# Selective scan of a 2D state-space layer: tiles of four states by 32 channels in place of two by 64, on one core

## The chip, the cores and the metric

The kernel runs on one core of a Trainium2 chip. The metric is the device time of one execution in microseconds. Five engines work side by side and meet only through semaphores: PE (TensorE, matrix products into PSUM), DVE (VectorE), ACT (ScalarE), POOL (GpSimd) and SP (SyncE, which here only issues DMAs, in the order of the program).

## The reference, cut to what matters

Two layers work on 8 images of 64 x 64 tokens with 192 channels. Layer 0 is not touched. Layer 1 projects to 384 channels, convolves, and runs a selective scan in four directions over the 4096 tokens. For each direction `k`, channel `d` and state `n` of 16:

```
x_dbl = x_proj_weight[k] @ xs[k]            # 12 rows for delta, 16 for B, 16 for C
delta = softplus(dt_projs_weight[k] @ x_dbl[:12] + dt_projs_bias[k])
A     = -exp(A_logs)
# per token l, sequential:
h[d, n] = exp(delta[d, l] * A[d, n]) * h[d, n] + (delta[d, l] * u[d, l]) * B[n, l]
y[d, l] = sum over n of h[d, n] * C[n, l]
ys      = y + u * Ds
```

The four directions (rows, columns, and both backwards) are summed, normalized over channels, gated and projected back. All arithmetic is in float32.

## The kernel before, in words

`layer1` handles one image after another. `front` (projection, convolution, stores of the result by channels and by tokens to DRAM, `xo`) and `finish` of the image before are interleaved by a planner; then `main` runs the scan of the image, which is the part that the change rewrites. Its order is written out by hand.

A **step** is one direction and one stretch of 512 tokens: 4 x 8 = 32 steps an image, 256 in all. A step has 24 **units**. A unit is two tiles `f` of 128 partitions by 512 tokens. Before the change a unit is `(p, d)`: `p` is a pair of the 16 states, `d` one of three groups of 128 channels, and each of the unit's two tiles holds 2 states x 64 channels. `ORDER` interleaves the eight `p`.

For each unit these are issued, unit `u` being the loop's index:

- `run(u)`: two scans on DVE (`tensor_tensor_scan`, line 1662) over decay `ea` and supply `g`, then on POOL a copy of the last column as the carry (`cy`, 1674) and the product of the states with C (`hs`, 1676; C is spread over partitions by DMA in the tile `cb`).
- `decay(u + 2)`: on ACT, two exponentials (1620) of `dr` (delta repeated over partitions by DMA) into `ea`, of which there are three buffers.
- `weigh`: on ACT (1605), delta times u, turned so that tokens lie on partitions (`duT`), is scaled with one state's B into `pw`; some are issued ahead for the next `p`.
- `supply(u + 1)`: on PE, `pw` is transposed into the PSUM tile `g` in blocks of 128 tokens (1646). For the first block of the four later `p`, `on_diagonal` holds: there, B has been laid on the diagonal of a 128 x 128 matrix `dg`, and a product of `duT` with it (1634) takes the place of `weigh` and transpose. `g` has four buffers.
- `collect(u - 2)`: on PE (1691), `sel` sums the product over the states of a tile into the PSUM tile `y`, 64 output channels at a time. In direction 0 the term `u * Ds` is added there too (`dskip`).
- `add(u - 3)`: on DVE (1700, 1702), after the last `p`, `y` goes into the image's sum.

Beside that, the pieces of `prepare(s + 1)` are issued at fixed units `q` of step `s`. At q = 0 `load` issues the DMAs of the next step's input, `xc` (1469) by channels and `ut` by tokens. At q = 2, 3, 4 `project` (1488) multiplies `xc` on PE, at q = 5 `keep` copies the result and stores C to DRAM (`cd`, 1497), and `spread` writes B to the diagonal of a DRAM matrix `dz` (1502) and reads it back as `dg` (1503). At q = 7 to 17 come delta (softplus on ACT), its transposes and `keep_du` (delta times u). `repeat_delta` (1587) spreads delta over the partitions of `dr`, at q = 11, 20 and 21, with four DMAs each. `load_c` (1593) is called at the first unit of each `p`, for the next `p`, with two DMAs into `cb`, of which there are three buffers.

All DMAs of the scan are issued by SP, in the order of the program. A DMA whose target buffer is still in use holds SP, and every DMA behind it, until it is free.

Of the kernel before, what the change touches and what calls it, by code (L numbers as in the profile page):

```python
# [29 lines left out]
NP1 = N // 2  # L30
ND = 8
ORDER = [0, 4, 1, 5, 2, 6, 3, 7]
# [1001 lines left out]
def layer1(tc, consts, x1s, mv1, out, w_in, w_x, w_dt, w_out):  # L1034
# [7 lines left out]
    with ExitStack() as ctx:  # L1042
# [17 lines left out]
        an = wp.tile([128, K, NP1, 2 * DT], F32, name="an")  # L1060
# [6 lines left out]
        sel = wp.tile([128, 64], F32, name="sel")  # L1067
        for i in range(2):
            nc.vector.tensor_copy(sel[i * 64 : i * 64 + 64], ident[i * 64 : i * 64 + 64, i * 64 : i * 64 + 64])
# [24 lines left out]
        zero = yacc[:, 0, : ND * 128].rearrange("p (n b) -> p n b", b=128)  # L1094
        nc.gpsimd.memset(zero, 0.0)
        dzs = [dgp.tile([ND, 128 * 128], F32, name=f"dz{i}") for i in range(2)]
        for t in dzs:
            nc.sync.dma_start(out=t.rearrange("n (a b) -> a n b", b=128), in_=zero)
# [343 lines left out]
        def scan(xo):  # L1442
# [11 lines left out]
            units = [(s, p, d) for s in range(len(steps)) for p in ORDER for d in range(DT)]  # L1454
# [6 lines left out]
            def prepare(s, bank=lambda name: mp.tile([128, TT], F32, name=name, tag="mm")):  # L1461
# [5 lines left out]
                def load():  # L1467
                    st["xc"] = pools["pr1"].tile([128, DT, TT], F32, name="xc")
                    o(nc.sync.dma_start(out=st["xc"], in_=xo[k % 2][:, :, c * TT : c * TT + TT]))
                    st["ut"] = pools["pr1"].tile([128, NB1, DIN], F32, name="ut", bufs=1)  # L1470
                    if k % 2 == 0:
                        src = xo[2][c * TT : c * TT + TT].rearrange("(j p) m -> p j m", p=128)
                        o(nc.sync.dma_start(out=st["ut"], in_=src))
                    else:
                        for i in range(2):
                            src = xo[2].rearrange("(h w) m -> w h m", w=WI)[c * RT + i : c * RT + RT : 2]
                            o(nc.sync.dma_start(out=st["ut"][i * 64 : i * 64 + 64], in_=src.rearrange("j h m -> h j m")))
                    if first(s):
                        st["wd"] = pools["pr1"].tile([45, DIN], F32, name="wd", bufs=1)
                        o(nc.sync.dma_start(out=st["wd"][32:45], in_=w_dt[k]))  # L1480
                    else:
                        st["wd"] = state[s - 1]["wd"]
# [16 lines left out]
                def spread():  # L1499
                    dz = dzs[s % 2]  # L1500
                    st["dg"] = dg = pools["dg1"].tile([128, ND, 128], F32, name="dg")
                    o(nc.sync.dma_start(out=dz[:, :: 128 + 1], in_=xds[s % 2][N - ND : N, 0:128]))
                    o(nc.sync.dma_start(out=dg, in_=dz.rearrange("n (a b) -> a n b", b=128)))
# [11 lines left out]
                def keep_b():  # L1515
                    st["bt"] = bt = pools["pr1"].tile([128, NB1, N], F32, name="bt")
                    o(nc.vector.tensor_copy(bt.rearrange("p a b -> p (a b)"), st["p_b"][:, : NB1 * N]))
                    st["duT"] = pools["pr1"].tile([128, NB1, DIN], F32, name="duT")
# [31 lines left out]
                def keep_du(d):  # L1550
                    o(
                        nc.vector.tensor_mul(  # L1552
                            st["duT"][:, :, d * 128 : d * 128 + 128],
                            st["p_du", d].rearrange("p (j t) -> p j t", j=NB1),
                            st["ut"][:, :, d * 128 : d * 128 + 128],
                        )
                    )
# [12 lines left out]
                    11: [(delta, 1), (turn, 0), (repeat_delta, s, 0)],  # L1570
# [5 lines left out]
                    17: [(keep_du, 2)],  # L1576
                    20: [(repeat_delta, s, 1)],
                    21: [(repeat_delta, s, 2)],
                }

            def repeat_delta(s, d):

                state[s]["dr", d] = dr = pools["dr1"].tile([128, 2, TT], F32, name="dr")
                de = state[s]["de", d]
                for f in range(2):
                    for i in range(2):
                        o(nc.sync.dma_start(out=dr[i * 64 : i * 64 + 64, f], in_=de[f * 64 : f * 64 + 64]))

            def load_c(s, p):
                state[s]["cb", p] = cb = pools["bc1"].tile([128, TT], F32, name="cb")  # L1590
                for i in range(2):
                    o(
                        nc.sync.dma_start(
                            out=cb[i * 64 : i * 64 + 64], in_=state[s]["cd"][2 * p + i].partition_broadcast(64)
                        )
                    )

            def weigh(s, p, j, i):

                st = state[s]  # L1600
                if i == 0:
                    st["pw", p, j] = pools["pw1"].tile([128, 2 * DT, 2, 64], F32, name="pw")
                n = 2 * p + i
# [3 lines left out]
                        st["duT"][:, j].rearrange("p (g c) -> p g c", c=64),  # L1607
# [5 lines left out]
            def decay(u):  # L1613
                s, p, d = units[u]
                k, c = steps[s]
                made["e", u] = ea = pools["e1"].tile([128, 2, TT], F32, name="ea")
                for f in range(2):
                    at = 2 * d + f
                    o(
                        nc.scalar.activation(  # L1620
                            ea[:, f], state[s]["dr", d][:, f], AF.Exp, scale=an[:, k, p, at : at + 1]
                        )
                    )

            def supply(u):
                s, p, d = units[u]
                gs = [pools["g1"].tile([128, TT], F32, name="g") for f in range(2)]
                made["g", u, 0], made["g", u, 1] = gs
                for j in range(NB1):
                    if on_diagonal(p, j):  # L1630
                        for f in range(2):
                            for i in range(2):
                                o(
                                    nc.tensor.matmul(  # L1634
                                        gs[f][i * 64 : i * 64 + 64, j * 128 : j * 128 + 128],
                                        state[s]["duT"][:, j, (2 * d + f) * 64 : (2 * d + f) * 64 + 64],
                                        state[s]["dg"][:, 2 * p + i - (N - ND)],
                                        start=True,
                                        stop=True,
                                    )  # L1640
                                )
                for f in range(2):
                    for j in range(NB1):
                        if not on_diagonal(p, j):
# [3 lines left out]
                                    state[s]["pw", p, j][:, 2 * d + f].rearrange("p a b -> p (a b)"),  # L1648
# [4 lines left out]
            def run(u):  # L1653
                s, p, d = units[u]
                k, c = steps[s]
                st = state[s]
                ea, g = made.pop(("e", u)), [made.pop(("g", u, f)) for f in range(2)]
                h = pools["h1"].tile([128, 2, TT], F32, name="hs")
                rev = (lambda ap: ap) if k < 2 else (lambda ap: ap[:, ::-1])
                for f in range(2):  # L1660
# [4 lines left out]
                            rev(g[f]),  # L1665
                            0.0 if first(s) else state[s - 1]["cy"][:, p, d, f : f + 1],
# [4 lines left out]
                if "cy" not in st:  # L1671
                    st["cy"] = pools["pr1"].tile([128, NP1, DT, 2], F32, name="cy")
                last = TT - 1 if k < 2 else 0
                o(nc.gpsimd.tensor_copy(st["cy"][:, p, d], h[:, :, last]))  # L1674
# [3 lines left out]
            def collect(u):  # L1678
                s, p, d = units[u]
                k, c = steps[s]  # L1680
                st = state[s]
                if p == ORDER[0]:
                    st["y", d] = pools["y1"].tile([128, TT], F32, name=f"y{d}")
                y = st["y", d]
                hc = made.pop(("hc", u))
                half = [slice(f * 64, f * 64 + 64) for f in range(2)]
                if p == ORDER[0] and k == 0:
                    for f in range(2):
                        o(nc.tensor.matmul(y[half[f]], dskip[:, d, half[f]], st["xc"][:, d], start=True, stop=False))
                for f in range(2):  # L1690
                    o(nc.tensor.matmul(y[half[f]], sel, hc[:, f], start=p == ORDER[0] and k > 0, stop=p == ORDER[-1]))  # L1691

            def add(u):
                s, p, d = units[u]
                k, c = steps[s]
                if p == ORDER[-1]:
# [7 lines left out]

            def on_diagonal(p, j):
                return j == 0 and 2 * p >= N - ND
# [4 lines left out]
                for p in ORDER  # L1711
                for j in range(NB1)
                for i in range(2)
# [3 lines left out]
            def prologue(f, mq, front_pools):  # L1717
# [3 lines left out]
                for name, n in (("pr1", 2), ("dr1", 4), ("pw1", 8), ("bc1", 3), ("e1", 3)):  # L1721
# [8 lines left out]
                r = yield step("DVE", 0.7, ready["keep"])  # L1730
                f.give("mm", r)
# [6 lines left out]
                load_c(0, ORDER[0])  # L1738
                for d in range(DT):
                    yield "wait", ("du", d)  # L1740
                for t in todo[:10]:
# [4 lines left out]
            def prologue_of(f, d):  # L1746
# [9 lines left out]
                yield step("SP", 0.1, lambda: repeat_delta(0, d), r)  # L1756
# [7 lines left out]
            def main():  # L1764
                for name, n, kw in (("dg1", 2, {}), ("h1", 6, {}), ("y1", 1, dict(space=PSUM)), ("g1", 4, dict(space=PSUM))):
                    spool(name, n, **kw)
                ready["spread"]()
                supply(0)
                rest = iter(todo[10:])
                nu = len(units)  # L1770
                for u, (s, p, d) in enumerate(units):
                    q = u % (NP1 * DT)
                    if q == 0:
                        pieces = prepare(s + 1) if s + 1 < len(steps) else {}
                    s2, p2, _ = units[u + DT - d] if u + DT - d < nu else (len(steps), 0, 0)
                    if s2 < len(steps) and d == 0:
                        load_c(s2, p2)
# [3 lines left out]
                    for _ in range(((2, 2, 2) if on_diagonal(p, 0) else (3, 3, 2))[d]):  # L1781
# [95 lines left out]
def _layout(i):  # L1877
# [15 lines left out]
    al = l1("A_logs").reshape(K, 2 * DT, 64, NP1, 2).transpose(4, 2, 0, 3, 1)  # L1893
# [39 lines left out]
```

## Time and profile before

| | |
|---|---|
| median of 3 runs | 23168.04 us (23161.08 to 23168.58) |
| profiled execution, its own time | 23175.73 us |
| its span | 23174.0 us |
| mean granted TensorE clock | 0.971 |
| instructions | 348545 |
| DMA packets | 1738653, 1998.38 MB |
| layer 0, and start of layer 1 (first scan of line 1662) | up to about 5023 us |
| scan loops of the 8 images | about 2030 us each |

The profile lists busy time for each engine, the span in slices, the DMA queues, the chain of work that ended last, and groups of instructions with their mean time. Matmuls overlap, so their mean time is longer than the distance from one to the next. SP is not counted as busy; what it does is read from the timeline, where its DMA issues stand as SPq.

### The profile page before, as it was taken

Reading aid. Unit: us, or ns where it says so; the run is one execution under the profiler, and the core shown is the slowest. Engines: PE = TensorE matmul, PEld = TensorE weight load, DVE = VectorE, ACT = ScalarE, POOL = GpSimd, SP = SyncE. Lnnn points to the kernel's source line nnn. Section 1 sums busy time; section 2 is a strip of 40 time slices with the busy share of each in tenths; the row PEclk is TensorE's granted clock in tenths of the full one; section 3 lists DMA queues with packets and bytes.
Section 4 is the critical chain, followed back from the end, with each engine's and each line's share of the span. In section 5 each row is a group of like instructions: output and inputs, shape, how many; then the busy total and the mean of one; then the engine's idle time right before and its main releaser. Section 6 shows DMA issues by size and latency. Waiting matters only on the chain.

```text
span 23174.0 us, 348545 instructions
## 1 busy us (share of the span) xinstructions
PE 21762.7 (94%) x118788; PEld 11070.5 (48%) x118788; DVE 21110.3 (91%) x22093; ACT 20048.9 (87%) x35418; POOL 16109.5 (70%) x12872
## 2 busy tenths in 40 slices
PE   8999999979998999899999999999999999999999
PEld 4444444435554555455545544554455445544554
DVE  7888888869998999899989998999899989998998
ACT  5666666759997999799979997999899989988998
POOL 1111111139995999599959995999599869976997
PEclk8999999989999999999999999999999999999999
DMA  1111111133333333333333334333433343333332
GB/s 52 45 44 41 45 45 45 42 96 92 95 93 111 92 92 94 111 94 93 90 114 93 92 87 117 95 92 88 117 92 92 89 117 93 93 91 113 92 94 75
DMA packets 1738653, 1998.38 MB, mean 86 GB/s; under 512 B 537280, under 2 KB 1034848, under 8 KB 1727648
## 3 DMA queue, kind: packets, MB, share of 16 engines
q1 hardware_dynamic: 1736864, 1976.07, 31.9%
q8 instruction: 934, 15.30, 0.3%
q14 instruction: 855, 7.00, 0.1%
HBM read 1360.20 MB, written 212.60 MB: 68 GB/s over the span
## 4 chain that ended last, share of the span: by engine, by line
PE 48%; ACT 22%; DVE 11%; POOL 8%; issue 6%; DMA 3%; SPq 2%; DVEq 0%; POOLq 0%; ACTq 0%
PE g L1646 10%; PE y L1691 10%; ACT ea L1620 10%; ACT pw L1605 9%; POOL hs L1676 7%; DVE hs L1662 3%; PE g L1634 3%; PE p_f L957 3%; DVE xs L1209 3%; PE p_d L1488 2%; PE p_x L450 2%; PE p_f L977 2%; PE p_dt L1523 2%; DMA dr<-de 2%; PE p_o L874 2%
## 5 line engine op out<-in xcount | busy, mean ns | idle before, releaser
L1676 POOL TENSOR_TENSOR hs<-hs,cb 128x1024 f32<-128x1024 f32 x6144 | 14584.3, 2374 | 496.4 <-POOL cy L1674 4.2
L1662 DVE TENSOR_TENSOR_SCAN hs<-ea,cy,g 128x512 f32<-128x512 f32 x10752 | 12894.9, 1258 | 187.2 <-PE g L1646 178.1
L1620 ACT ACTIVATE ea<-dr,an 128x512 f32<-128x512 f32 x12288 | 8139.8, 710 | 528.5 <-DVE hs L1662 507.0
L1605 ACT ACTIVATE pw<-duT,bt 128x384 f32<-128x384 f32 x14336 | 7832.7, 600 | 23.5 <-DVE duT L1552 23.5
L1691 PE MATMUL y<-hs,sel 128*64 128x512 f32 x24576 | 6635.2, 618 | 360.0 <-POOL hs L1676 338.6
L1646 PE MATMUL g<-ident,pw 128*128 128x128 f32 x43008 | 6089.9, 281 | 41.1 <-ACT pw L1605 4.8
L1646 PEld LDWEIGHTS g<-ident,pw 128*128 128x128 f32 x43008 | 4612.5, 141 | 2522.6 <-issue 1254.9
L1674 POOL COPY cy<-hs 128x2 f32<-128x2 f32 x6144 | 1160.7, 189 | 2262.0 <-DVE hs L1662 2228.8
L1634 PEld LDWEIGHTS g<-dg,duT 128*64 128x64 f32 x24576 | 1557.4, 136 | 2053.0 <-issue 1484.6
L1634 PE MATMUL g<-dg,duT 128*64 128x128 f32 x24576 | 2257.9, 282 | 169.4 <-DVE hs L1662 106.1
L1691 PEld LDWEIGHTS y<-hs,sel 128*64 128x64 f32 x24576 | 1234.2, 135 | 1563.0 <-issue 865.6
L1662 DVE TENSOR_TENSOR_SCAN hs<-ea,g 128x512 f32<-128x512 f32 x1536 | 1751.8, 1197 | 129.1 <-PE g L1646 116.8
L367 POOL TENSOR_TENSOR s<-xs 96x512 f32<-96x512 f32 x64 | 121.7, 1902 | 2139.6 <-DVE xs L345 1850.2
L1523 PE MATMUL p_dt<-xdbl,wd 13*128 13x512 f32 x1536 | 857.5, 639 | 96.2 <-DVE duT L1552 71.0
L1209 DVE SCALAR_TENSOR_TENSOR xs<-pad,p,xs 128x4096 f32<-128x4096 f32 x192 | 860.9, 4484 | 50.7 <-ACT xs L1199 43.5
L367 POOL TENSOR_TENSOR s<-sq 96x512 f32<-96x512 f32 x128 | 180.1, 1407 | 942.7 <-ACT sq L380 864.4
L1488 PE MATMUL p_d<-xc,wx 128*44 128x512 f32 x1536 | 788.6, 596 | 19.9 <-DMA xc<-xo 19.9
L957 PE MATMUL p_f<-h,wf 96*128 96x512 f32 x1536 | 762.4, 635 | 44.1 <-ACT zs L552 27.5
L345 DVE SCALAR_TENSOR_TENSOR x<-xx,p,x 96x512 f32<-96x512 f32 x1024 | 784.8, 816 | 15.2 <-ACT x L334 15.0
L345 DVE SCALAR_TENSOR_TENSOR xs<-xin,p,xs 96x512 f32<-96x512 f32 x1024 | 746.1, 768 | 3.6 <-ACT xs L334 3.6
L977 PE MATMUL p_f<-m,wf 128*96 128x512 f32 x1536 | 696.1, 604 | 0.0
L1545 PEld LDWEIGHTS p_du<-ident,de 128*128 128x128 f32 x3072 | 323.9, 141 | 610.1 <-DVE de L1536 406.3
(205 smaller groups left out, 19972.1 us busy)
## 6 DMA issues: line engine op xcount, KB each, us to landing
cb<-cd SPq DMA_DIRECT2D x4096, 128.0 KB
dr<-de SPq DMA_DIRECT2D x3072, 128.0 KB
xc<-xo SPq DMA_DIRECT2D x256, 768.0 KB
dg<-dz SPq DMA_DIRECT2D x256, 512.0 KB
e<-csd SPq DMA_DIRECT2D x256, 384.0 KB
xl<-x SPq DMA_DIRECT2D x256, 384.0 KB
ut<-xo SPq DMA_DIRECT2D x128, 768.0 KB
ut<-xo SPq DMA_DIRECT2D x256, 384.0 KB
```

Of the source, the lines that this page charges most:

```text
L345: nc.vector.scalar_tensor_tensor(im(out[:, ct]), tap(ct, j), w[:, ct, j : j + 1], im(out[:, ct]), ALU.mult, ALU.add)
L957: nc.tensor.matmul(ps, wf1[:, ct, mt * 128 : mt * 128 + 128], h[:, ct], start=ct == 0, stop=ct == 1)
L1209: nc.vector.scalar_tensor_tensor(xs, tap(j), kw[:, d, j : j + 1], xs, ALU.mult, ALU.add)
L1488: nc.tensor.matmul(st["p_d"][:44], wx[:, d, k], st["xc"][:, d], start=d == 0, stop=d == DT - 1)
L1523: nc.tensor.matmul(ps, st["wd"][32:45, d * 128 : d * 128 + 128], xds[s % 2][32:45], start=True, stop=True)
L1605: nc.scalar.activation(st["pw", p, j][:, :, i], st["duT"][:, j].rearrange("p (g c) -> p g c", c=64), AF.Copy, scale=st["bt"][:, j, n : n + 1],
L1620: nc.scalar.activation(ea[:, f], state[s]["dr", d][:, f], AF.Exp, scale=an[:, k, p, at : at + 1])
L1634: nc.tensor.matmul(gs[f][i * 64 : i * 64 + 64, j * 128 : j * 128 + 128], state[s]["duT"][:, j, (2 * d + f) * 64 : (2 * d + f) * 64 + 64], ...
L1646: nc.tensor.transpose(gs[f][:, j * 128 : j * 128 + 128], state[s]["pw", p, j][:, 2 * d + f].rearrange("p a b -> p (a b)"), ident,)
L1662: nc.vector.tensor_tensor_scan(rev(h[:, f]), rev(ea[:, f]), rev(g[f]), 0.0 if first(s) else state[s - 1]["cy"][:, p, d, f : f + 1], ALU.mu ...
L1676: o(nc.gpsimd.tensor_mul(h, h, bc(st["cb", p], 1, [128, 2, TT])))
L1691: o(nc.tensor.matmul(y[half[f]], sel, hc[:, f], start=p == ORDER[0] and k > 0, stop=p == ORDER[-1]))
```

## The change

A tile now holds 4 states x 32 channels. A unit is `(p, g)`: `p` one of four groups of four states (in plain order), `g` one of six groups of 64 channels, so there are still 24 units of two tiles in a step.

- `supply`: the diagonal is used for one of the four token blocks of `p` = 0 and 2 and for two of them for `p` = 1 and 3 (six of the sixteen pairs of `p` and block, before: four of 32). A tile's diagonal block is made of four products of 32 columns, at column positions 0, 32, 64 and 96, in place of two of 64.
- `weigh` writes four states of 32 channels; the number of its calls in a step is 64 less 4 for each block on a diagonal.
- `collect` works on every second unit: four products with a `sel` of 32 columns, side by side, give 128 channels of `y`.
- `repeat_delta` is called for each of six `g`, at q = 17 to 22, with eight DMAs of 32 partitions each; `dr` has six buffers.
- `load_c` is called for each of four `p`, at units 0, 6, 12 and 18 for the `p` after; it issues four DMAs of 32 partitions into `cb` (now two buffers), and one or two DMAs for `dg`, which is no longer read in `spread`.
- `spread` writes 16 rows of the first block's diagonal and twice four of the second's, in three DMAs. `ut` is gone: `load` reads into `duT`, and `keep_du` multiplies in place.

```diff
-            units = [(s, p, d) for s in range(len(steps)) for p in ORDER for d in range(DT)]
+            units = [(s, p, g) for s in range(len(steps)) for p in range(NQ1) for g in range(NG)]
...
-                    st["dg"] = dg = pools["dg1"].tile([128, ND, 128], F32, name="dg")
-                    o(nc.sync.dma_start(out=dz[:, :: 128 + 1], in_=xds[s % 2][N - ND : N, 0:128]))
-                    o(nc.sync.dma_start(out=dg, in_=dz.rearrange("n (a b) -> a n b", b=128)))
+                    for j, dz in enumerate(dzs[s % 2]):
+                        for p in range(j, NQ1, j + 1):
+                            n = slice(0, N) if j == 0 else slice(4 * p, 4 * p + 4)
+                            o(nc.sync.dma_start(out=dz[n, :: 128 + 1], in_=xds[s % 2][n, j * 128 : j * 128 + 128]))
+                            if j == 0:
+                                break
...
-                    11: [(delta, 1), (turn, 0), (repeat_delta, s, 0)],
+                    11: [(delta, 1), (turn, 0)],
...
-                    17: [(keep_du, 2)],
-                    20: [(repeat_delta, s, 1)],
-                    21: [(repeat_delta, s, 2)],
+                    17: [(keep_du, 2), (repeat_delta, s, 0)],
+                    **{17 + g: [(repeat_delta, s, g)] for g in range(1, NG)},
...
-            def repeat_delta(s, d):
+            def repeat_delta(s, g):
...
                 for f in range(2):
-                    for i in range(2):
-                        o(nc.sync.dma_start(out=dr[i * 64 : i * 64 + 64, f], in_=de[f * 64 : f * 64 + 64]))
+                    at = (2 * (g % 2) + f) * 32
+                    for i in range(4):
+                        o(nc.sync.dma_start(out=dr[i * 32 : i * 32 + 32, f], in_=de[at : at + 32]))
...
+                for i in range(4):
+                    o(nc.sync.dma_start(out=cb[i * 32 : i * 32 + 32], in_=st["cd"][4 * p + i].partition_broadcast(32)))
+                st["dg", p] = dg = pools["dg1"].tile([128, 2, 4, 128], F32, name="dg")
+                for j in range(p % 2 + 1):
+                    src = dzs[s % 2][j][4 * p : 4 * p + 4].rearrange("n (a b) -> a n b", b=128)
+                    o(nc.sync.dma_start(out=dg[:, j], in_=src))
...
+                            for i in range(4):
                                 o(
                                     nc.tensor.matmul(
-                                        gs[f][i * 64 : i * 64 + 64, j * 128 : j * 128 + 128],
-                                        state[s]["duT"][:, j, (2 * d + f) * 64 : (2 * d + f) * 64 + 64],
-                                        state[s]["dg"][:, 2 * p + i - (N - ND)],
+                                        gs[f][i * 32 : i * 32 + 32, j * 128 : j * 128 + 128],
+                                        st["duT"][:, j, at : at + 32],
+                                        st["dg", p][:, j, i],
                                         start=True,
                                         stop=True,
+                                        tile_position=(0, i * 32),
                                     )
                                 )
...
+                hc = [made.pop(("hc", u - 1)), made.pop(("hc", u))]
+                for i in range(4):
+                    o(
+                        nc.tensor.matmul(
+                            y[i * 32 : i * 32 + 32],
+                            sel,
+                            hc[i // 2][:, i % 2],
+                            start=p == 0 and k > 0,
+                            stop=p == NQ1 - 1,
+                            tile_position=(0, i * 32),
+                        )
+                    )
...
             def on_diagonal(p, j):
-                return j == 0 and 2 * p >= N - ND
+                return j <= p % 2
...
-                for name, n in (("pr1", 2), ("dr1", 4), ("pw1", 8), ("bc1", 3), ("e1", 3)):
+                for name, n in (("pr1", 2), ("dr1", 6), ("pw0", 3), ("bc1", 2), ("e1", 3), ("dg1", 2)):
...
-                    s2, p2, _ = units[u + DT - d] if u + DT - d < nu else (len(steps), 0, 0)
-                    if s2 < len(steps) and d == 0:
-                        load_c(s2, p2)
+                    if g == 0 and u + NG < nu:
+                        load_c(*units[u + NG][:2])
                     run(u)
                     if u + 2 < nu:
                         decay(u + 2)
-                    for _ in range(((2, 2, 2) if on_diagonal(p, 0) else (3, 3, 2))[d]):
+                    for _ in range(((1, 1, 2, 2, 1, 1), (1, 2, 3, 2, 2, 2))[p % 2][g]):
                         if t := next(rest, None):
                             weigh(*t)
```

## The prediction

> **What bounds the kernel now.** I read first the busy times of the page, then a stretch in the middle of a scan, then the timeline there, and last what SP waits for.
>
> ```profile
> PE 21762.7 (94%) x118788; PEld 11070.5 (48%) x118788; DVE 21110.3 (91%) x22093; ACT 20048.9 (87%) x35418; POOL 16109.5 (70%) x12872
> ```
>
> Over the span PE looks busiest. Inside the scan (windows: for each engine busy us and instructions) it is DVE:
>
> ```profile
> core 0: us, PE busy (x) PEld busy (x) DVE busy (x) ACT busy (x) POOL busy (x), PEclk, DMA share, GB/s
> 8500.00:9000.00 500.00, 482.61 (x3088) 252.16 (x3084) 495.51 (x471) 491.51 (x878) 480.72 (x383) 1.00 0.36 94
> ```
>
> DVE is idle 0.9% of this stretch. From the starts of every 48th scan in the trace, a step lasts 62.9 us in directions 1 to 3 and 65.2 us in direction 0; the idle time before DVE's instructions is 0.34 and 2.34 us of these. So DVE's own work is 62.56 us a step (62.86 in direction 0): a floor, since the change leaves DVE 48 scans and 11 other instructions. POOL's 24 pairs of carry and product, 2.585 us from one to the next, make 62.0. All idle of DVE in the 256 steps is about 349 us, 1.5% of the time: no more can be gained.
>
> Then the timeline, first SP's issues (start, us from the first's start to the last's end, number):
>
> ```profile
> 8517.49 0.59 SPq L1469 DMA_DIRECT2D xc<-xo  x1
> 8536.00 0.33 SPq L1497 DMA_DIRECT2D cd<-xdbl  x1
> 8536.38 0.32 SPq L1502 DMA_DIRECT2D dz<-xdbl  x1
> ```
>
> and, near the end of that step, all engines:
>
> ```profile
> 8568.27 16.50 DVE L1662 TENSOR_TENSOR_SCAN hs<-ea,cy,g 128x512 f32<-128x512 f32 x14
> ...
> 8572.11 2.41 SPq L1587 DMA_DIRECT2D dr<-de  x4
> 8573.48 0.87 PE L1646 MATMUL g<-ident,pw 128*128 128x128 f32 x6
> 8574.28 1.08 PE L1691 MATMUL y<-hs,sel 128*64 128x512 f32 x4
> 8574.61 1.18 SPq L1593 DMA_DIRECT2D cb<-cd  x2
> 8575.19 0.70 PE L1634 MATMUL g<-dg,duT 128*64 128x128 f32 x8
> 8575.90 3.23 SPq L1587 DMA_DIRECT2D dr<-de  x4
> 8579.24 1.19 SPq L1593 DMA_DIRECT2D cb<-cd  x2
> 8580.47 0.60 SPq L1469 DMA_DIRECT2D xc<-xo  x1
> ...
> 8589.49 0.12 PEld L1488 LDWEIGHTS p_d<-xc,wx 128*44 128x44 f32 x1 [0.28 <-issue]
> ```
>
> The two `xc` loads are one step apart (62.98 us). A unit of two scans takes 16.50/7 = 2.36 us. The last `xc` is issued behind eight `dr` and four `cb` DMAs; in nine steps that I followed in the records it landed 5.2 to 6.9 us after its issue began, here 5.2, at 8585.7, and its first product's weights load on PE at 8589.49: 3.8 us to spare. Back to back, DMAs of 64 partitions end 0.64 us apart, whatever they carry (`dr` after `dr`, `cb` after `cb`, `xc` after `cb`, all 0.64 in the issue records). And SP is not free to run ahead:
>
> ```profile
> SPq L1593 <- POOL cy L1674: 4308.7, 1033, 7.6
> ```
>
> (SP's waits: total us, times, longest): `cb` loads wait for POOL to be done with the buffer.
>
> **The change, part by part.**
>
> *ACT.* A step's `weigh` calls fall from 56 to 40. One costs 7832.7 us / 14336 = 0.55: 8.7 us a step less. DVE is the floor, so this is worth only what it saves of DVE's idle. The weights are now finished just before the first `supply` of a `p`: at the end of a step two `weigh` (1.1 us) follow `decay` (1.32) before a transpose (0.17 + 0.3) may run, 2.9 us against a unit of 2.36: up to 0.6 us, four places a step, three of them beside a 0.66 us extra on DVE. I take 0.3 a step, outside the stall below.
>
> *PE.* Pairs of 64 columns run as one: in the records their starts are 7 ns apart, and the next round follows 0.109 us later (128 columns) or 0.43 (512). A tile's diagonal block is two rounds, 0.22, a transpose 0.109. If four groups of 32 run as one, such a block stays at two rounds; 48 more blocks in place of 48 transposes cost 48 x 0.11 = 5.3 us a step, and `collect` falls from 24 to 12 times (0.86 + 0.2 for the switch of shape): -12.7. PE gains 7 us, off the path except in direction 0, where its extra sums cause the 2 us of idle. If four run two at a time the block is 0.44 and `collect` 1.72: see the second rival. The nearest row (pairs do not queue at all) is why I take four at once. The Trainium skill (TensorEngine Tiling (Array Packing), Tiling Modes) also lists four independent tiles of 128 x 32; no run here shows them yet.
>
> *`keep_du`, the carry, the adds, `ut`:* the same instructions with the same shapes; nothing. SP's wait of 3.3 us between `dz` and `dg` goes; SP was idle then.
>
> *SP.* This is the step that decides. DMAs a step: `dr` 12 to 48, `cb` 16 to 16, `dg` 1 to 6, `dz` 1 to 3. Their order around the step's end is now: `dr` of g 0; at unit 18 `load_c` for the next step's `p` 0 (4 `cb`, 1 `dg`); five times eight `dr`; at the next step's unit 0 `load_c` for `p` 1 (4 `cb`, 2 `dg`); only then `xc`. `cb` has two buffers now, so the load at unit 18 waits until POOL has done unit 17, which in the records of before is 2.9 us after that unit's scan ends, i.e. after the start of unit 18. From there 48 DMAs of 32 partitions and three `dg` (0.43 each, 0.386 plus the gap) come ahead of `xc`.
>
> What does one DMA of 32 partitions take on SP? No row shows one. From below: a `dz` behind the 16-partition `cd` ends 0.37 us after it; the shortest single issue of all, 0.305, with its gap 0.35. From above: 0.64, the same DMAs of 64 partitions. By partitions the form lies between, so I take the middle, 0.50. (The data bound each lower: 2 KB packets from SBUF to SBUF take 166 ns on each of 16 engines, two each, 0.33 us.) The Trainium skill (DMA: Bandwidth & Descriptors, Issuing engines are not separate DMA queues) holds the time to initiate a DMA to be usually small beside the DMA itself; by that rule the 0.33 of data would bind and the stall below would be 2.4 us before the catching up. The rows say otherwise: 0.64 from issue to issue for `cb`, whose 64 packets need 4 x 84 ns = 0.34.
>
> So `xc` is issued at 2.9 + 48 x 0.50 + 1.3 = 28.2 us after the start of unit 18 and lands at 33.5 (5.3 later, near the low end, because the DMAs just ahead of it are half as large). PE meets `project` in unit 2 of the next step and stands there, with all later `supply` behind it. DVE still has the units up to 3; unit 4 needs a product (0.95) and a supply (1.25) after the landing: 35.7. Without a stall unit 4 would start ten units and three extras after unit 18: 10 x 2.34 + 3 x 0.63 = 25.3. DVE stands 10.4 us a step. PE has then lost its lead, and the two other products (0.95 + 0.2) meet a `collect` before the next supplies: 1.5 more. Sum 11.9. `dr` of g 5 lands near 27 and delays only what waits anyway; the weights' stall at the step's end is covered too.
>
> Per step: 62.56 + 11.9 = 74.5 in place of 62.9 (+11.6), in direction 0 74.8 in place of 65.2 (+9.6; the 2 us that PE cost there are hidden or gone). The loads are made in 31 of an image's 32 steps: 8 x (23 x 11.6 + 8 x 9.6) = 2750 us. Eight prologues with 36 more DMAs each add perhaps 5 us each, 40. The profiled execution took 23175.73 us, its span 23174.0, 8 us above the median of the runs: 23168 + 2790 = about 25950.
>
> With 0.37 a DMA the stall is 4.2 + 1.5 = 5.7: +5.4 and +3.4 a step, 8 x (23 x 5.4 + 8 x 3.4) = 1210, about 24380. With 0.64 it is 17.1 + 1.5: +18.3 and +16.3, 4410, about 27600.
>
> **The rivals.**
>
> *The queue keeps up, and the change is faster.* Place: `xc` at unit 2. The point: 25.3 - 2.9 - 1.3 - 5.3 - 2.2 = 13.6 us for 48 DMAs, 0.28 each. For it: with smaller packets spread out, `xc` could land in 3.4 us rather than 5.3, POOL could be done earlier, and the point moves to 0.33. Against it: no issue in the trace is shorter than 0.305 plus its gap. Price: direction 0 loses its 2 us of idle (64 x 2.0 = 128) and the others 0.2 (192 x 0.2 = 40): 23000.
>
> *PE takes the groups of 32 columns two at a time.* Then a unit costs PE, for even `p`, 0.87 + 0.66 + 0.86 and 0.4 of switches = 2.79, for odd 1.74 + 0.44 + 0.86 + 0.4 = 3.44: 74.8 a step, with 6.8 for the pieces of `prepare` 81.6. 192 x 18.7 + 64 x 16.4 = 4640: 27800; the longer units would hide most of SP's lag. Nothing but the missing row speaks for it.
>
> *The change cancels out:* a stall of 1 us from a queue just over its point, paid by what PE and ACT save: 23170.
>
> **How the numbers follow.** What a measurement of this kernel can tell from no change is about 0.2%, 46 us. Chances: forecast 0.80, PE two at a time 0.08, faster 0.09, cancelling 0.03. So slower 0.88. The range takes the bounds of the DMA's cost, 24380 to 27600, stretched below for a landing or an anchor 1 to 2 us earlier and above to the second rival: 23900 to 27800. Faster and cancelling are left out, and a part of the second rival.
>
> **What would show it.** In the changed profile: `xc<-xo` issued some 25 us after unit 18's `load_c` and well inside unit 4 of the step rather than before unit 0; between them 40 `dr` issues in an almost unbroken row, whose distance is my 0.50; a large wait of `p_d` on the DMA `xc`, and of DVE's scan on PE, near 10 us a step; ACT down to some 80% busy and below; the `y` products in rounds of four, 7 ns apart. Wrong would be: no wait at `p_d`; a step of 62.6; or PE without gaps at 80 us a step. If DMAs of 32 partitions go at 0.37 or 0.64, the mechanism stands and the size goes to an end of the range.

## The result, and the profile after

| | before | after |
|---|---|---|
| median of the runs | 23164.56 us (23155.18 to 23168.58) | 29382.35 us (29373.93 to 29398.22) |
| ratio, 95% interval | | 1.2686 (1.2664 to 1.2708) |
| span of the profiled execution | 23174.0 us | 29378.8 us |
| mean granted TensorE clock | 0.971 | 0.866 |
| a step, median, directions 1 to 3 / direction 0 | 62.9 / 65.2 us | 88.6 / 88.9 us |
| DVE idle in the scans and just ahead of each image's first, whole run | 349 us | 6370 us |

The kernel is 27% slower. The forecast had the sign and the place, but not the size: 25950, with a range to 27800. The steps account for all of it: 8 x (23 x 25.7 + 8 x 23.7) = 6246 us, beside 6205 us more span. And idle time of DVE accounts for nearly all of that, 6021 us.

The busy times of the page, changed kernel:

```profile
PE 21624.5 (74%) x228996; PEld 11626.7 (40%) x228996; DVE 21279.1 (72%) x22095; ACT 18383.6 (63%) x31322; POOL 16200.0 (55%) x12872
```

Against the page of before, DVE works as long (21279 and 21110 us), PE too, and ACT 1665 us less. Every share fell because the span grew: no engine is the bound any more, something that engines wait for is. The same stretch as before (windows: busy us and instructions of each engine):

```profile
core 0: us, PE busy (x) PEld busy (x) DVE busy (x) ACT busy (x) POOL busy (x), PEclk, DMA share, GB/s
8500.00:9000.00 500.00, 337.29 (x4610) 190.35 (x4602) 355.10 (x334) 313.18 (x532) 345.62 (x273) 0.86 0.35 88
```

DVE was idle for 0.9% of this stretch, now for 29%, and the DMA engines are no busier (0.36 before, 0.35 now). What fills the time is not bytes. SP's timeline of one step and the start of the next (start, us from the first's start to the last's end, number) shows what does:

```profile
8518.69 1.72 SPq L1594 DMA_DIRECT2D cb<-cd  x4
8520.50 0.38 SPq L1598 DMA_DIRECT2D dg<-dz  x1
8520.98 26.44 SPq L1588 DMA_DIRECT2D dr<-de  x40
8547.52 1.92 SPq L1594 DMA_DIRECT2D cb<-cd  x4
8549.54 0.93 SPq L1598 DMA_DIRECT2D dg<-dz  x2
8550.52 0.59 SPq L1469 DMA_DIRECT2D xc<-xo  x1
8551.15 0.61 SPq L1473 DMA_DIRECT2D duT<-xo  x1
...
8570.14 3.72 SPq L1503 DMA_DIRECT2D dz<-xdbl  x3
...
8609.28 26.81 SPq L1588 DMA_DIRECT2D dr<-de  x40
...
8639.19 0.59 SPq L1469 DMA_DIRECT2D xc<-xo  x1
```

This is the row that the forecast asked for: forty `dr` issues without a break, then `cb` and `dg` for `p` = 1, then `xc`; the next `xc` is 88.67 us later. Forty take 26.44 us, 0.66 each. What follows on the other engines (timeline of the changed kernel; in brackets the idle time before, and who ended it):

```profile
8558.06 1.93 PE L1488 MATMUL p_d<-xc,wx 128*44 128x512 f32 x2 [20.29 <-DMA xc<-xo]
...
8559.92 1.08 PE L1638 MATMUL g<-dg,duT 128*32 128x128 f32 x16
...
8560.94 1.54 PE L1651 MATMUL g<-ident,pw 128*128 128x128 f32 x6
8561.98 2.45 DVE L1667 TENSOR_TENSOR_SCAN hs<-ea,cy,g 128x512 f32<-128x512 f32 x2 [20.21 <-PE g L1651]
...
8564.48 1.06 PE L1488 MATMUL p_d<-xc,wx 128*44 128x512 f32 x2
8565.46 0.65 PE L1638 MATMUL g<-dg,duT 128*32 128x128 f32 x16
8566.03 0.64 PEld L1651 LDWEIGHTS g<-ident,pw 128*128 128x128 f32 x6 [0.20 <-issue]
8566.04 0.87 PE L1651 MATMUL g<-ident,pw 128*128 128x128 f32 x6
8566.72 2.45 DVE L1667 TENSOR_TENSOR_SCAN hs<-ea,cy,g 128x512 f32<-128x512 f32 x2 [2.29 <-PE g L1651]
```

PE stands 20.29 us at `project` for `xc`; DVE's unit 4 stands as long for the `supply` queued behind it on PE, and unit 5 another 2.29. The waits of the whole run (total us, times, longest) say that this is the case in every step:

```profile
DVE hs L1667 <- PE g L1651: 5878.2, 1220, 23.5
...
PE p_d L1488 <- DMA xc<-xo: 5004.3, 256, 24.8
```

One part of the forecast that concerned PE can be read from the groups (busy us, mean ns of one; first after, then before):

```profile
L1698 PE MATMUL y<-hs,sel 128*32 128x512 f32 x24576 | 3511.6, 641 | 32.8 <-POOL hs L1681 32.3
```

```profile
L1691 PE MATMUL y<-hs,sel 128*64 128x512 f32 x24576 | 6635.2, 618 | 360.0 <-POOL hs L1676 338.6
```

The same number of products in about half the time: four groups of 32 columns do run as one, and the rival in which PE takes them two at a time is out.

### The profile page after: what moved, and what is told of

The parts are those of the page before. It is cut to its first block, busy times and chain, and to the rows that moved or that the text cites. A ratio compares the mean times of both kernels' runs of the same rounds, so it can differ in the third digit from the quotient of the medians.

```text
span 29378.8 us, 582734 instructions
## 1 busy us (share of the span) xinstructions
PE 21624.5 (74%) x228996; PEld 11626.7 (40%) x228996; DVE 21279.1 (72%) x22095; ACT 18383.6 (63%) x31322; POOL 16200.0 (55%) x12872
## 4 chain that ended last, share of the span: by engine, by line
PE 31%; SPq 19%; POOL 17%; DVE 9%; DMA 9%; ACT 9%; issue 6%; POOLq 0%; ACTq 0%; DVEq 0%
SPq L1588 16%; POOL hs L1681 16%; DMA xc<-xo 7%; PE g L1638 5%; ACT ea L1622 4%; PE g L1651 4%; PE p_d L1488 3%; DVE hs L1667 3%; PE y L1698 3%; ACT pw L1607 3%; PE p_f L956 2%; DVE xs L1209 2%; SPq L1594 2%; PE p_x L449 2%; POOL cy L1679 1%
## 5 line engine op out<-in xcount | busy, mean ns | idle before, releaser
L1622 ACT ACTIVATE ea<-dr,an 128x512 f32<-128x512 f32 x12288 | 8288.7, 713 | 8171.4 <-DVE hs L1667 5355.0
L1651 PE MATMUL g<-ident,pw 128*128 128x128 f32 x30720 | 5116.8, 296 | 1259.3 <-ACT pw L1607 1259.3
L1638 PE MATMUL g<-dg,duT 128*32 128x128 f32 x147456 | 5691.8, 284 | 437.7 <-DVE hs L1667 340.2
L1607 ACT ACTIVATE pw<-duT,bt 128x384 f32<-128x384 f32 x10240 | 5755.3, 600 | 32.0 <-DVE duT L1553 32.0
L1638 PEld LDWEIGHTS g<-dg,duT 128*32 128x32 f32 x147456 | 3932.9, 113 | 3857.1 <-issue 2736.1
L1488 PE MATMUL p_d<-xc,wx 128*44 128x512 f32 x1536 | 1032.4, 762 | 5004.3 <-DMA xc<-xo 5004.3
L1651 PEld LDWEIGHTS g<-ident,pw 128*128 128x128 f32 x30720 | 3440.3, 147 | 2735.5 <-ACT pw L1607 1472.1
L1698 PE MATMUL y<-hs,sel 128*32 128x512 f32 x24576 | 3511.6, 641 | 32.8 <-POOL hs L1681 32.3
L1488 PEld LDWEIGHTS p_d<-xc,wx 128*44 128x44 f32 x1536 | 138.3, 134 | 5361.8 <-DMA xc<-xo 5053.4
L1698 PEld LDWEIGHTS y<-hs,sel 128*32 128x32 f32 x24576 | 495.7, 110 | 724.0 <-issue 557.4
```

Of the source, the lines that this page charges most:

```text
L1488: nc.tensor.matmul(st["p_d"][:44], wx[:, d, k], st["xc"][:, d], start=d == 0, stop=d == DT - 1)
L1607: nc.scalar.activation(st["pw", p, j][:, :, i], st["duT"][:, j].rearrange("p (g c) -> p g c", c=32), AF.Copy, scale=st["bt"][:, j, n : n + 1],
L1622: nc.scalar.activation(ea[:, f], state[s]["dr", g][:, f], AF.Exp, scale=an[:, k, p, at : at + 1])
L1638: nc.tensor.matmul(gs[f][i * 32 : i * 32 + 32, j * 128 : j * 128 + 128], st["duT"][:, j, at : at + 32], st["dg", p][:, j, i], start=True, ...
L1651: nc.tensor.transpose(gs[f][:, j * 128 : j * 128 + 128], st["pw", p, j][:, 2 * g + f].rearrange("p a b -> p (a b)"), ident,)
L1698: nc.tensor.matmul(y[i * 32 : i * 32 + 32], sel, hc[i // 2][:, i % 2], start=p == 0 and k > 0, stop=p == NQ1 - 1, tile_position=(0, i * 32),)
```

## The experiments

Step times are medians over directions 1 to 3. DVE's idle time is a mean over the same steps, sorted by the unit in whose turn it falls; this sorting gives 20.7 us at unit 4 for the changed kernel, 1.3 at unit 5, 3.4 elsewhere, 25.4 in all. Ratios are to runs of the kernel before beside them.

| | us | ratio (95%) | step | DVE idle a step |
|---|---|---|---|---|
| after | 29382.35 | 1.2686 (1.2664 to 1.2708) | 88.6 | 25.4 |
| e1 `xc` a step ahead | 26419.06 | 1.1410 (1.1391 to 1.1429) | 76.0 | 13.0 |
| e2 half the `dr` DMAs | 26178.76 | 1.1306 (1.1289 to 1.1323) | 75.3 | 12.5 |
| e3 before, with 32-partition `dr` | 23608.06 | 1.0199 (1.0184 to 1.0214) | 64.5 | 2.2 |
| e4 `xc` ahead, `dr` by DRAM | 23795.04 | 1.0279 (1.0264 to 1.0294) | 65.8 | 2.9 |
| e5 `xc` before `cb` and `dg` | 28036.14 | 1.2104 (1.2087 to 1.2120) | 82.7 | 19.8 |
| e6 e1 and e2 together | 23797.56 | 1.0270 (1.0256 to 1.0284) | 65.8 | 2.9 |
| e7 e4, weights earlier | 23285.38 | 1.0053 (1.0040 to 1.0067) | 63.8 | 1.0 |

The theory: the forty-odd DMAs that SP issues one by one ahead of `xc` are the loss. The rivals: that it is the bytes of `dr`, or PE's or ACT's new work in itself.

**e1: only the place of `xc` in SP's order.**

```diff
+            def load_x(s):
...
+                    state[s]["xc"] = xc = pools["pr1"].tile([128, DT, TT], F32, name="xc")
+                    o(nc.sync.dma_start(out=xc, in_=xo[k % 2][:, :, c * TT : c * TT + TT]))
...
-                    st["xc"] = pools["pr1"].tile([128, DT, TT], F32, name="xc")
-                    o(nc.sync.dma_start(out=st["xc"], in_=xo[k % 2][:, :, c * TT : c * TT + TT]))
...
-                    16: [(turn, 2)],
+                    16: [(turn, 2), (load_x, s + 1)],
```

> The changed kernel, with the next step's xc load alone moved: it is issued at unit 16 of the step before, ahead of all dr loads, in place of unit 0. Theory (SP's queue of small DMAs makes xc late, PE stands at project, DVE runs dry at unit 4): the 20 us of DVE's idle at unit 4 go. Next in line is dr itself: its 40 loads end 33 us after unit 18's start, the scan of unit 29 is due at 27.7 and needs 1.5 us of exponentials, so some 7 us of idle a step are left, now at units 3 to 6 and on the wait for dr. Step 88.6 to about 71, total about 25,000. PE's clock rises. Rival (PE: the 147456 narrow products and their drains, or the clock): the position of one load changes nothing, the step stays at 85 or more, total above 28,500.

Measured: 26419, a step of 76.0. The 20.7 us at unit 4 fell to 1.8, so the wait for `xc` was what held unit 4. But a step is 5 us above the 71 expected: idle time stands at units 5, 6 and 7 now (2.5, 4.2, 1.2). The waits name the next customers of the same queue:

```profile
ACT ea L1628 <- DMA dr<-de: 2819.8, 1778, 4.1
...
PE g L1644 <- DMA dg<-dz: 2006.0, 373, 11.0
DVE hs L1673 <- PE g L1657: 1925.9, 1320, 15.4
```

ACT waited as long for `dr` in the changed kernel (2787.2 us), but there DVE stood for `xc` at the same time. Without that stall the last groups of `dr` come late first: before the scans of units 4 and 5 DVE waits mostly for ACT's exponentials. Behind `dr` stand the `cb` and `dg` of `p` = 1, and `dg`, needed at unit 6, comes late next: PE waits 2006 us for it, where the changed kernel has 85. Taking one customer out of a late queue moves the wait to the next.

**e2: half as many DMAs, the same bytes.**

```diff
-                    at = (2 * (g % 2) + f) * 32
-                    for i in range(4):
-                        o(nc.sync.dma_start(out=dr[i * 32 : i * 32 + 32, f], in_=de[at : at + 32]))
+                    at = (g % 2) * 64
+                    for i in range(2):
+                        o(nc.sync.dma_start(out=dr[i * 64 : i * 64 + 64, f], in_=de[at : at + 64]))
```

> The changed kernel, with dr filled by four DMAs of 64 partitions for each g in place of eight of 32: the same bytes and the same destination, half as many DMAs (the rows are those of the layout before, so delta belongs to other channels than it should; nothing else is left out). Theory: a DMA costs SP 0.64 to 0.66 us whatever its size, so the chain from unit 18 to xc is shorter by 20 x 0.65 = 13 us and DVE's idle at unit 4 falls from 20 to 5 to 7 us, a little more with PE's clock: step about 74, total about 25,700. Rival (the data: 3 MB a step of dr at 166 ns for each 2 KB packet on 16 engines): no change, step 88, total above 29,000.

Measured: 26179, a step of 75.3, 8.0 us at unit 4. The twenty `dr` ahead of `xc` took 13.7 us (median) in place of 26.8 for forty: the same bytes, half the time. It is the number of DMAs that costs here, not what they carry.

**e3: the kernel before, with the DMAs of after.** Only `dr` is cut into 24 DMAs of 32 partitions in place of 12 of 64.

```diff
-                        o(nc.sync.dma_start(out=dr[i * 64 : i * 64 + 64, f], in_=de[f * 64 : f * 64 + 64]))
+                        for h in range(2):
+                            at = i * 64 + h * 32
+                            src = f * 64 + h * 32
+                            o(nc.sync.dma_start(out=dr[at : at + 32, f], in_=de[src : src + 32]))
```

> The kernel before, with one part of the change done alone: dr is filled by eight DMAs of 32 partitions for each d in place of four of 64, the same bytes. Theory: the two dr loads ahead of xc take 2 x 4 x 0.65 = 5.2 us more, xc is issued at 3.3 us after the step's start in place of 1.9 before and lands at about 8.6; PE comes to project at 7.6 and has about a microsecond of lead there, so the kernel is near its deciding point: 0 to 1.5 us a step, total 23,165 to 23,540. Rival (narrow DMAs cost by themselves, through the DMA engines or the buffers' ports): more than 2 us a step, above 23,700.

Measured: 23608, 2.0% slower, +1.6 us a step, slightly past the upper end expected. SP's timeline of this kernel shows the price of a form that no row of before had:

```profile
8535.22 4.98 SPq L1590 DMA_DIRECT2D dr<-de  x8
8540.30 1.78 SPq L1596 DMA_DIRECT2D cb<-cd  x2
8542.18 4.97 SPq L1590 DMA_DIRECT2D dr<-de  x8
8547.25 1.18 SPq L1596 DMA_DIRECT2D cb<-cd  x2
8548.48 0.59 SPq L1469 DMA_DIRECT2D xc<-xo  x1
```

Eight take 4.98 us, 0.62 each; from the end of one to the end of the next it is 0.63 (median), where the DMAs of 64 partitions took 0.64. Eight more of them stand ahead of `xc` than before, 5.0 us; the 3.8 us that `xc` had to spare cover most of it, and DVE begins to stand (0.6 us at each of units 4 and 5).

**e4: the queue emptied.** As e1; and `de` is written to DRAM by twelve DMAs, whenever it is ready, with its four repeats, so that each `dr` is one load of 128 partitions: 18 DMAs in place of 48, six of them in the place of the forty-eight.

```diff
-                        o(nc.sync.dma_start(out=dr[i * 32 : i * 32 + 32, f], in_=de[at : at + 32]))
+                o(nc.sync.dma_start(out=dr, in_=state[s]["dd"][g].rearrange("i c f t -> (i c) f t")))
+            def store_delta(s, d):                               # at q = 10, 12, 15
+                ...
+                        o(nc.sync.dma_start(out=state[s]["dd"][g, :, :, f].rearrange("i c t -> c i t"),
+                                            in_=de[at : at + 32].unsqueeze(1).to_broadcast([32, 4, TT])))
```

> The changed kernel with xc moved as in the first run of this batch and dr made by 18 DMAs a step in place of 48: each 32 rows of delta are stored four times to DRAM (12 DMAs, at units 10, 12 and 15), and one DMA of 128 partitions loads each g (6, at the units where they were). Theory: SP's chain around the step's end is some 12 DMAs, nothing waits for it, DVE is at its floor of 62.6 us but for up to 0.6 us of idle where the weights are finished late; direction 0 loses its 2 us. Total 23,050 to 23,200, PE's clock as before. Rival (PE, narrow products): PE would now be the bound and the step 65 or more, total above 23,700.

Measured: 23795, a step of 65.8. 90% of the loss is gone, so it was the queue. But the kernel stayed 2.8% slower than before where no loss or a small gain was expected: 2.9 us a step of idle remain, at units 12 (1.0), 0 and 1 (0.7), 9, 13 and 11. The waits of PE before its transposes point at ACT's weights, and they are as long as in the changed kernel (1472.1 and 1259.3 us there), so moving the DMAs did not touch them:

```profile
PEld g L1667 <- ACT pw L1623: 1510.9, 1135, 3.1
PE g L1667 <- ACT pw L1623: 1267.8, 837, 2.9
```

**e5: the landing by itself.** At unit 0, `load` (with `xc`) is called before `load_c` in place of after it. Nothing else changes.

```diff
+                    for f, *args in pieces.pop(0, ()) if q == 0 else ():
+                        f(*args)
                     if g == 0 and u + NG < nu:
                         load_c(*units[u + NG][:2])
```

> The kernel after with the order of two calls at unit 0 swapped: the next step's load (xc, duT) is issued before the four cb and two dg of p = 1. Theory (what the forecast left out is the landing: the dg block of 512 KB in 512-byte packets lies directly ahead of xc in the queues): xc is issued 2.8 us earlier (4 cb at 0.46 and two dg at 0.48) and its first product follows in about 5.5 us in place of 7.9, so unit 4 idles about 15 us in place of 20.0, a step takes about 83.4 in place of 88.6: about 28,100 us. Rival (the 7.9 comes from the forty dr before it, or from PE): only the 2.8 us are won, a step 85.8, about 28,700.

Measured: 28036, a step of 82.7, 15.0 us at unit 4, as the theory had it. In the records `xc` is issued 31.7 us after unit 18's start in place of 34.9, and PE's first product follows 5.7 us after the issue in place of 7.9 (medians). One step of this run, SP's issue and PE's first product:

```profile
8531.79 0.59 SPq L1469 DMA_DIRECT2D xc<-xo  x1
8536.94 1.94 PE L1488 MATMUL p_d<-xc,wx 128*44 128x512 f32 x2 [13.60 <-DMA xc<-xo]
```

The forty `dr` stand ahead of `xc` in both kernels, so they are not what made the landing slow. By order alone it could be `cb` or `dg`; the records of the DMA packets tell them apart. In the changed kernel the 1024 packets of 512 bytes of the `dg` block (512 KB) start only after `xc`'s issue, in nearly every step, and the last of them 2.2 us after it (median); in e5 there is none in that time. These are the 2.2 us.

**e6: e1 and e2 together.**

> xc issued a step ahead (as in e1) and dr by DMAs of 64 partitions, 24 a step in place of 48 (as in e2; this spreads the same bytes, but delta of other channels). Theory (what is left of e1's idle is the same queue, for its later customers dr, cb and dg): the idle of units 4 to 7 goes, what stays is that of the weights at the borders of p, some 2.5 us: a step of 65 to 66, about 23,700 us. Rival (e1's rest is not SP's: PE behind ACT, or a switch of shapes): e1's 76.0 falls by little, a step over 72, above 25,300.

Measured: 23798, a step of 65.8. Each alone had left 12.5 to 13 us of idle a step; together they leave 2.9, and those at the same units as e4, although e4's transfers go another way. So what is left in both is not SP's.

**e7: the weights earlier.** As e4, with the changes below; `delta`, `turn`, `keep_du`, `step` and `store_delta` are placed anew around the two `soft`.

```diff
-                    for _ in range(((1, 1, 2, 2, 1, 1), (1, 2, 3, 2, 2, 2))[p % 2][g]):
+                    for _ in range(((2, 2, 2, 2, 0, 0), (2, 3, 3, 3, 1, 0))[p % 2][g]):
                         if t := next(rest, None):
                             weigh(*t)
...
-                    10: [(soft, 1), (store_delta, s, 0)],
...
-                    13: [(soft, 2)],
...
+                    12: [(soft, 1)],
...
+                    15: [(soft, 2)],
```

> As e4 (xc a step ahead, dr by stores to DRAM and six loads), and the weigh calls of each p moved ahead in it, with the softplus of the second and third channel group moved from units 10 and 13 to 12 and 15, so that the weights of a p are finished one to two units before its first supply. Theory (what is left of e4's idle, 2.9 us a step, are mostly weights late at units 12, 13, 0 and 1): 1.5 to 2.4 us a step go, a step of 63.4 to 64.3, 23,200 to 23,450 us. Rival (the idle is that of PE and the DMAs, or ACT's exponentials now come late in its place): no change or slower, 23,700 and above.

Measured: 23285, a step of 63.8: the idle at units 0, 1, 11 and 12 is gone, 1.0 us a step remains. Weights and softplus were moved together, so the run does not tell what each is worth. The same stretch of the trace as above (windows):

```profile
core 0: us, PE busy (x) PEld busy (x) DVE busy (x) ACT busy (x) POOL busy (x), PEclk, DMA share, GB/s
8500.00:9000.00 500.00, 456.30 (x6448) 256.61 (x6447) 490.75 (x465) 426.46 (x738) 474.77 (x379) 0.98 0.60 168
```

DVE is at 98% again, with ACT 65 us and PE 26 us less busy than before in these 500 us. So the change does free ACT and PE. It gains nothing by it: DVE's own work in a step is 62.8 us here, and a step of before takes 62.9. The kernel is still 0.5% slower than before; no version here beats before, and the 349 us of idle that before has are the most there was to win.

## Why the prediction was wrong in size

**Right.** The place (`xc`, at `project` in unit 2, seen by DVE at unit 4), the order of the queue, the anchor (the first `cb` is issued 2.5 us after unit 18's start; 2.9 in the forecast), the catching up at unit 5 (1.3; 1.5), ACT (the `weigh` calls took 7832.7 us and take 5755.3, 8.1 a step less; 8.7 in the forecast) and PE's groups of 32. e1 and e5 show the place, e2 and e3 the number of DMAs as the cause.

**Wrong: the size.** The step was put at 74.5 and is 88.6, 14.1 more. Term by term (medians, idle times as means; the last column adds up to 14.1):

| term | forecast | measured | more |
|---|---|---|---|
| 40 `dr` at 0.50 | 20.0 | 26.8 (0.67 each) | 6.8 |
| 8 `cb` and 3 `dg`, anchor | 8.2 | 8.0 | -0.2 |
| from `xc`'s issue to its first product | 5.3 | 7.9 | 2.6 |
| product and supply, to unit 4's scan | 2.2 | 3.9 | 1.7 |
| units 18 to 3 without the stall (comes off) | 25.3 | 25.9 | -0.6 |
| catching up at unit 5 | 1.5 | 1.3 | -0.2 |
| small idles at other units (0.3 held to be covered) | 0 | 3.4 | 3.4 |
| DVE's own work | 62.6 | 63.2 | 0.6 |

*The price of a DMA* is the step that failed first. I chose the middle, 0.50, by partitions, between 0.37 and 0.64. The row nearest in kind, `dr` itself at 64 partitions and 0.64, was the right one: e3 has 0.62 for half the partitions, and e2 0.69 for 64 in a row of twenty. Only `cb`, from DRAM, became cheaper with fewer partitions (0.64 to about 0.47). The upper bound, 0.64, was passed because some issues in a long row take 1 to 2 us (4 in 100 of all `dr`; the median distance is 0.63). The rule of the Trainium skill that the forecast cites (DMA: Bandwidth & Descriptors, Issuing engines are not separate DMA queues) would by the forecast's own sum have put the stall at 2.4 us before the catching up; the trace has 20.7.

*The landing.* The forecast took 5.3 us because the DMAs just ahead were "half as large". It had counted SP's time for the two `dg` reads, 0.43 each, and not what they put on the DMA engines. e5 and the packets show that this alone was 2.2 us.

*Product and supply* were taken at full speed from a trace in which PE never stands for long. Two windows at the end of the stall shown above (columns as before; the third last is the granted clock):

```profile
8558.40:8562.50 4.10, 4.10 (x25) 2.16 (x24) 0.52 (x1) 0.00 (x0) 0.00 (x0) 0.50 0.04 14
8562.50:8585.00 22.50, 22.09 (x292) 11.09 (x295) 17.73 (x18) 15.54 (x27) 15.60 (x14) 0.99 0.17 27
```

After 20 us without work PE was granted half its clock (0.50) for these 4.1 us, which are the ones on the path: the pair of `p_d` products takes 1.93 us and then 1.06 six us later, the transposes 1.54 and 0.87. From the product to DVE's scan it is 3.92 us for unit 4 (8558.06 to 8561.98) and 2.24 for unit 5 (8564.48 to 8566.72), the 2.2 of the forecast. The Trainium skill (TensorE: Matmul & The Clock Gate, What's actually happening) has the half clock after a window of some 3.4 us without work, until a window of work has passed. The two windows fit it; no run here tests the length of that window. A forecast of a stall should have priced the work behind it at half speed.

*The small idles.* "The weights' stall at the step's end is covered too" was wrong: the stall stands at unit 4, and the weights are late at units 0 and 1, ahead of it, and at 12 and 13, a third of a step behind it, where it hides nothing. Units 9 and 11 have another 0.9 us, of which the kernel before has 0.55 too. e4 and e6 show 2.9 us a step of small idles without the stall, e7 that 1.9 go when softplus and weights are moved.

The range failed with it. The price of the DMA alone, 6.8 us in 8 x 31 steps, would have made 25950 + 1690 = 27640, still inside the range. But the range's upper end moved this price alone and left landing, supply and the small idles at one value each; these three, 7.7 us a step, took the result out of it.

**What stays open:** why SP needs 0.63 us for a DMA from SBUF to SBUF at 32 partitions as at 64, while 32 partitions from DRAM take 0.47; and why DVE's own work is 0.2 to 1.1 us a step longer in all changed kernels.

## What to carry to other kernels

A tile of more repeats and fewer channels multiplies the DMAs that build it; count every issue on the queue between two loads, price it by the row of the same kind (source, target), not by its size, and ask which load with a near customer stands last. When a queue is late, list all its customers in order of their need: moving the first one only shows the second. A stall on PE costs its own length and then, as here, the half clock on the very work that ends it (3.9 us in place of 2.2), so bound each term of such a sum, not the dearest alone.

## What the runs showed of the hardware

- A DMA from SBUF to SBUF in a row of its kind holds SP for 0.62 to 0.69 us, whether it moves 64 KB over 32 partitions (0.62 in e3, 0.67 in the changed kernel) or 128 KB over 64 (0.64 before, 0.69 in e2).
- A load of 768 KB right behind 512 KB in 512-byte packets was used 7.9 us after its issue, one ahead of them 5.7 us (e5).
- Three `dz` DMAs, which write single elements to a diagonal, hold SP for 3.72 us in a row, where the one of before shows 0.32. Hardly anything waits for them here.
